# GNN layer on one core: the second lane's sort placed behind the first lane's matmuls, sums stored by SyncE, the quad loop written out

## The chip, the core and the metric

The kernel runs on one core of a Trainium2 chip. The metric is the device time of one execution in microseconds (us). The kernel before took 24514.12 us (median of ten runs, 24499.75 to 24533.43). A difference of 0.2% is about what these runs can tell from no change.

## The reference

A graph layer over V = 100,000 nodes with 64 features and 3,300,000 edges (`src`, `dst`, sorted by `dst`, self loops included):

```python
h = jnp.maximum(_layernorm(x, axis=-1), 0.0)
local = features[tgt]; nbr = features[src]          # features = h
y = concat([local, nbr - local], -1) @ W.T + b
s = segment_sum(y, tgt);  cnt = segment_sum(1, tgt)
x = x + where(cnt > 0, s / maximum(cnt, 1), 0)
```

Since the map is linear, what has to be made per node is the sum of `h[src]` over its edges and the number of edges; the matrix is applied afterwards, once per node.

## The kernel before

**Stages.** (1) Preparation: layer norm of all nodes; each row of h is stored in DRAM as three bf16 parts and two ones (`h3`, 194 columns, 388 bytes), and a sum table `acc` is zeroed. (2) Edge sums, two ways at once, added into `acc`. (3) Per node: mean, matrix, output (lines 976 to 1019).

**Way one, chunks** (`chunks`, L343 to 412): 352 chunks of 128 x 28 edges. For each of the 28 columns one indirect DMA on GpSimd (POOL), a "gather", brings 128 rows of `h3` into a tile `nb` (L391): 9856 gathers in all. VectorE (DVE) makes one-hots `hot` of the edges' targets, 14 columns at a time and 128 targets wide (L340 through `one_hot`), and TensorE (PE) multiplies them with the rows, one matmul for each gather (L396), into 128 node sums. DVE takes the sums out (L407, L409), and POOL adds them to `acc` in DRAM: with an indirect DMA (L366) before the loop and with a direct accumulating DMA (L371) inside it.

**Way two, windows and quads.** The other 2,039,808 edges lie in 256 windows of 7968 edges, each over at most 256 neighbouring targets. Four windows make a quad; 32 quads (128 windows, one per partition) make a lane; there are two lanes, so 64 quads. For a lane, `sort_lane` (L413 to 617) sorts the keys of each partition by source block: pieces of up to 1536 key pairs, each a copy on ScalarE (ACT) into a PSUM tile `tmp` (L455), then a minimum and a maximum on DVE (L456, L457). `fill_lane` (L620 to 738) then fetches the sorted keys in small pieces with 225 POOL gathers (L636, L721), and DVE and ACT turn them into index tables in DRAM. `quads` (L740 to 881) works through 157 source blocks of 640 rows for each quad, two blocks at a step, 79 steps a quad: SyncE (SP) loads the block table `tab` (L761, 727.5 KB for three blocks) and the indices `srs`, `dt`; DVE makes the one-hots `gh` (L789) and `dh` (L340); PE picks rows out of the block (`pick`, 12 matmuls a step, L811); ACT moves them to SBUF (`gs`, L813); PE adds them up by target (`put`, 32 small matmuls a step, L819). At a quad's end ACT and DVE make four tiles `wsums` (L835 to 845), and POOL adds them to `acc` with accumulating DMAs (L849).

**What sets the order.** Instructions are ordered on each engine by a scheduler that takes the earliest written instruction that is ready; `issue_after` holds one behind another. Work is interleaved by Python generators: `gathers(ns)` emits one gather for each `GATHER` = 1250 ns of credit (`took()` takes credit off for a gather of `fill_lane`). Lane 0 is sorted with gathers beside it; lane 1 is sorted with gathers and lane 0's fill beside it; quads 0 to 3 run with lane 1's fill and gathers; `drain(ev)` finishes the first 58 chunks (L909); then a hardware loop (`For_i`, L911) runs three times over 20 quads and 98 chunks. An addition to `acc` isn't issued at once: `add_later` files it, and `add_now` issues it some gathers later (56 gathers, then at least `GAP` = 8 apart). A register for its address is first loaded on the issuing engine (`number`, L318).

Of the kernel before, what the change touches and what calls it, by code (L numbers as in the profile page):

```python
# [32 lines left out]
LANES = 2  # L33
SB = 20
KB = 98
U0 = 4
KG = 16
# [3 lines left out]
STEP = 1050  # L41
GAP = 8
# [19 lines left out]
PIECE = 1536  # L62
COUNTS = 1
GAIN = 2.0 ** 40
PART = 1024
# [19 lines left out]
def plan(v, e):  # L85

    wl = 1 << int(np.log2(33 * CH * 1.05))
    ew = wl - PAD
    nw = LANES * P
    chunks = -(-(e - nw * ew) // CHUNK)  # L90
    return wl, nw, max(chunks, (nw // W - U0) // SB * KB)


@with_exitstack
def gnn_preln(ctx: ExitStack, tc, x, src_w, dst_w, src_p, dst_p, src_a, dst_a, wT, b, out, V, E):
# [27 lines left out]
    SETS = NL * G  # L123
# [7 lines left out]
    PA = NCH - (SETS - U0) // SB * KB  # L131
# [4 lines left out]
    assert 2 * C == P and NCB % 2 == 1 and PA >= 0 and SL % 2 == 0  # L136
# [9 lines left out]
    wb_d = dram.tile([SETS * W, 1], I32, name="wb_d")  # L146
# [28 lines left out]
    wb_r = consts.tile([1, SETS * W], I32, name="wb_r")  # L175
    turns = consts.tile([1, 2], I32, name="turns")
    ones = consts.tile([P, 1], F32, name="ones")
# [4 lines left out]
    odd = consts.tile([P, 1 + 5 * LANES], F32, name="odd")  # L182
# [22 lines left out]
    with tc.tile_pool(name="pre", bufs=2) as pre, tc.tile_pool(name="small", bufs=4) as small, \  # L205
# [32 lines left out]
        most = small.tile([P, NMT], F32, name="most", bufs=1)  # L238
        nc.vector.memset(least, 0.0)
        nc.vector.memset(most, 0.0)  # L240

        def bounds(m):
# [3 lines left out]
            nc.vector.tensor_reduce(least[:n, m:m + 1], d[:n], axis=AX.X, op=ALU.min)  # L246
            if m == NMT - 1:

                nc.vector.scalar_tensor_tensor(d[:n], d[:n], float(V), d[:n], op0=ALU.is_lt, op1=ALU.mult)
            nc.vector.tensor_reduce(most[:n, m:m + 1], d[:n], axis=AX.X, op=ALU.max)  # L250
            if m < NMT - 1:
                return
            span = small.tile([P, NMT], F32, name="span", bufs=1)
            nc.vector.tensor_sub(span, most, least)
            nc.vector.tensor_reduce(odd[:, 0:1], span, axis=AX.X, op=ALU.max)
            nc.vector.tensor_scalar(odd[:, 0:1], odd[:, 0:1], float(P), None, op0=ALU.is_ge)
# [55 lines left out]
    with tc.tile_pool(name="rows", bufs=6) as rows, \  # L312
# [5 lines left out]
        def number(at, engine, most):  # L318
            with tc.issue_after(last[engine].ins):
                return nc.values_load(at, engines=[engine], min_val=0, max_val=most)  # L320
# [5 lines left out]
        later = []  # L326
        count = [0, 0]
# [4 lines left out]
        def add_now(all_of_them=False):  # L332
            while later and (all_of_them or (later[0][0] <= count[0] and count[0] - count[1] >= GAP)):
                later.pop(0)[1]()
                count[1] = count[0]

# [8 lines left out]
        def chunks(first, n, dynamic=None):  # L345


            def load(q):
# [7 lines left out]
                nc.vector.tensor_sub(rel[:, :k], di[:, :k], base_b[:, at][:, :, None].to_broadcast([P, k, J]))  # L356
                near = index.tile([P, KG, J, D], I16, name="near")
                nc.vector.tensor_scalar(near[:, :k], rel[:, :k, :, None].to_broadcast([P, k, J, D]), float(2 * CH), None,
                                        op0=ALU.min)
                to = index.tile([P, KG], I32, name="to", bufs=3)  # L360
                nc.vector.tensor_scalar(to[:, :k], base_b[:, at], pcol, None, op0=ALU.add)
                return si, near, to

            def addition(q, rows_to, sums):
                if dynamic is None:
                    nc.gpsimd.indirect_dma_start(  # L366
                        out=acc, out_offset=bass.IndirectOffsetOnAxis(ap=rows_to, axis=0),
                        in_=sums, in_offset=None, compute_op=ALU.add)
                else:
                    at = number(base_r[0:1, ds(dynamic + q, 1)], POOL, V)  # L370
                    nc.gpsimd.dma_start(acc[ds(at, P)], sums, accum_op=ALU.add)  # L371

            ahead = load(0)
            before = None
            parts = J // JH
            for k in range(n * parts + 1):
                q, part = divmod(k, parts)
                u = q % KG
                if q < n:
                    if u == 0 and part == 0:  # L380
                        si, near, to = ahead
                    hot = rows.tile([P, JH, P], BF16, name="hot", bufs=4)
                    nb = rows.tile([P, JH, CT], BF16, name="nb")
                    with behind():
                        one_hot(hot, near[:, u, part * JH:part * JH + JH], P)
                if before is not None and before[2] == 0:
                    ps = rows_ps.tile([P, CE], F32, name="ps")
                for j in range(JH):
# [6 lines left out]
                    if before is not None:  # L395
                        nc.tensor.matmul(ps, lhsT=before[0][:, j], rhs=before[1][:, j, :CE],  # L396
# [7 lines left out]
                if before is not None and before[2] == parts - 1:  # L404
                    sums = rows.tile([P, C1], F32, name="sums", bufs=LAG + 2)
# [4 lines left out]
                    add_later((LAG - 1) * J, lambda b=before[3], s=sums: addition(*b, s))  # L410
                if q < n:
                    before = (hot, nb, part, (q, to[:, u:u + 1]))
# [5 lines left out]
        def sort_lane(l, keys, piece, few, ps):  # L418

            whole = keys.bitcast(I32)  # L420
# [3 lines left out]
            nc.vector.tensor_scalar_min(wb[:, 0:1], wb[:, 0:1], float(V - CH))  # L424
            last[DVE] = nc.vector.tensor_reduce(wb[:, 1:2], whole[:, :EW], axis=AX.X, op=ALU.max)
# [6 lines left out]
            mine = slice(l * P, l * P + P)  # L432
            for i in range(W):
                nc.sync.dma_start(wb_d[mine].rearrange("(g i) o -> i g o", i=W)[i], wb_i[i * G:i * G + G])
            nc.sync.dma_start(wb_r[:, mine], wb_d[mine].rearrange("w o -> o w"))
            for a in range(0, EW, PART):
# [12 lines left out]
                last[DVE] = nc.vector.scalar_tensor_tensor(d, d, 1, s[:, :n],  # L449
                                               op0=ALU.logical_shift_left, op1=ALU.bitwise_or)  # L450
# [3 lines left out]
            def exchange(lo, hi, tmp):  # L454
                last[ACT] = nc.scalar.copy(tmp, lo)  # L455
                nc.vector.tensor_tensor(lo, tmp, hi, ALU.min)  # L456
                last[DVE] = nc.vector.tensor_tensor(hi, tmp, hi, ALU.max)  # L457
# [601 lines left out]
```

## Time and profile before

| What | us |
|---|---|
| Median of ten runs | 24514.12 |
| The profiled execution: its time | 24535.56 |
| Its span in the trace | 24533.9 |
| Lane 0's sort: first key fetch of its fill | 1649 |
| First `gh` one-hot of quad 0 | 2726 |
| First and last quad sums before the loop | 3290, 4080 |
| First gather sums added inside the loop | 4379 |
| Last quad's sums taken out of PSUM | 24196 |
| End of the span | 24534 |

The trace is read in windows of time. In each, a row gives the busy time of each engine with the number of its instructions in brackets, then the TensorE clock that was granted (1 is full), the busy share of the DMA engines and GB/s. PE is matmuls, PEld weight loads. A group row gives the line, the engine, the operation, the number of instructions, busy time and mean ns of one, and, after the bar, the idle time of the engine just before them with what ended it. "issue" means that nothing that the profile shows was being waited for.

### The profile page before, as it was taken

What the parts mean: (1) busy time and instruction counts of PE and PEld (TensorE: products, weight loads), DVE (VectorE), ACT (ScalarE), POOL (GpSimd) and SP (SyncE); (2) the same over time, 40 slices, a digit from 0 to 9 for tenths busy, and PEclk for the clock granted to TensorE, in tenths of its full rate; (3) what the DMA queues carried; (4) which work ended last, traced back from release to release, by engine and by line L of the source; (5) the groups of instructions that cost most, each with busy time, mean ns of one, the idle gap of its engine ahead of it and who ended that gap; (6) DMA issues with size and microseconds to landing.
All of it is one profiled execution on the core that took longest, in us unless ns stands there. A gap on an engine that the chain in (4) does not pass through costs nothing. (4 is left out here: it accounts for less than half of the span.)

```text
span 24533.9 us, 559362 instructions
## 1 busy us (share of the span) xinstructions
PE 15201.9 (62%) x238778; PEld 10912.5 (44%) x238778; DVE 11304.8 (46%) x15452; ACT 6034.7 (25%) x11710; POOL 11122.7 (45%) x11210
## 2 busy tenths in 40 slices
PE   4100365666666666657666666666576666766666
PEld 3000244444444444445444444444454444444445
DVE  6879543444444444434444444444344444444444
ACT  4333321222222222222222222222222222222222
POOL 5666534444444444434444444444344444444444
PEclk6555577777777777777777777777777777777777
DMA  6612364555555555555555555555555555555557
GB/s 234 102 43 48 102 176 149 174 176 175 175 172 175 175 178 174 175 158 180 175 175 176 176 171 175 175 175 176 159 180 174 175 176 175 175 177 176 173 174 252
DMA packets 1746424, 4097.89 MB, mean 167 GB/s; under 512 B 943899, under 2 KB 952230, under 8 KB 1738950
## 3 DMA queue, kind: packets, MB, share of 16 engines
q1 hardware_dynamic: 1182534, 3461.26, 41.7%
q0 software_dynamic: 454208, 535.92, 11.1%
q10 hardware_dynamic: 107168, 64.74, 1.2%
q8 instruction: 1877, 30.75, 0.5%
q14 instruction: 637, 5.22, 0.1%
HBM read 3880.72 MB, written 219.04 MB: 167 GB/s over the span
## 5 line engine op out<-in xcount | busy, mean ns | idle before, releaser
L391 POOL DMA_INDIRECT nb<-h,si x9856 | 9421.0, 956 | 11738.0 <-PE ps L396 8031.2
L819 PE MATMUL total<-gs,dh 32*128 32x193 bf16 x160768 | 6608.8, 266 | 4278.0 <-issue 4254.3
L340 DVE TENSOR_TENSOR dh<-dt,c 128x1024 bf16<-128x1024 int16 x5056 | 3451.5, 683 | 11992.5 <-remote 7483.2
L813 ACT CAST gs<-gp 128x386 bf16<-128x386 f32 x10048 | 4761.2, 482 | 16234.3 <-remote 9614.5
L811 PE MATMUL gp<-tab,gh 128*128 128x193 bf16 x60288 | 7498.7, 274 | 1976.7 <-issue 1751.6
L811 PEld LDWEIGHTS <-gh 128*128 128x128 bf16 x60288 | 5490.3, 106 | 3666.4 <-issue 3242.8
L819 PEld LDWEIGHTS <-dh 32*128 32x128 bf16 x160768 | 3943.3, 99 | 6624.1 <-issue 6562.4
L789 DVE TENSOR_TENSOR gh<-srs,c 128x1536 bf16<-128x1536 int16 x5056 | 4764.2, 942 | 23.9 <-issue 18.3
L396 PE MATMUL ps<-nb,hot 128*128 128x193 bf16 x9856 | 1940.6, 280 | 2633.4 <-DVE sums L409 1220.7
L396 PEld LDWEIGHTS <-hot 128*128 128x128 bf16 x9856 | 1045.9, 111 | 2808.2 <-DVE sums L409 1252.9
L455 ACT COPY tmp<-keys 128x1536 f32<-128x1536 f32 (+14 forms) x540 | 649.9, 1213 | 1281.2 <-issue 568.5
L456 DVE TENSOR_TENSOR keys<-tmp,keys 128x1536 f32<-128x1536 f32 (+14 forms) x540 | 757.0, 1423 | 88.0 <-ACT junk L533 35.9
L457 DVE TENSOR_TENSOR keys<-tmp,keys 128x1536 f32<-128x1536 f32 (+14 forms) x540 | 757.1, 1422 | 14.0 <-remote 7.1
L340 DVE TENSOR_TENSOR hot<-near,c 128x1792 bf16<-128x1792 int16 x704 | 760.2, 1080 | 2.8 <-PE ps L396 2.7
L849 POOL DMA_DIRECT2D acc<-wsums x256 | 347.4, 1357 | 326.9 <-DVE wsums L845 219.0
L636 POOL DMA_INDIRECT kf<-ksort,at_i x322 | 309.1, 960 | 200.1 <-ACT k L677 105.4
L371 POOL DMA_DIRECT2D acc<-sums x294 | 300.9, 1023 | 209.9 <-DVE sums L409 200.6
L839 DVE SCALAR_TENSOR_TENSOR whole<-own,whole 128x193 f32<-128x193 bf16 x512 | 191.2, 416 | 178.5 <-ACT whole L835 178.0
L778 POOL DMA_INDIRECT rows_x<-h,xs x128 | 123.3, 963 | 324.7 <-DMA xs<-xs_d 262.0
L407 DVE TENSOR_REDUCE sums<-ps 128x64 f32<-128x192 f32 x352 | 123.8, 352 | 226.9 <-remote 168.5
L303 PE MATMUL o_ps<-w_own,hT 128*128 128x128 f32 x784 | 186.3, 376 | 15.1 <-ACT hT L298 14.6
L303 PEld LDWEIGHTS o_ps<-w_own,hT 128*128 128x128 f32 x784 | 154.9, 252 | 80.9 <-ACT hT L298 71.1
(174 smaller groups left out, 3522.4 us busy)
## 6 DMA issues: line engine op xcount, KB each, us to landing
tab<-tables SPq DMA_DIRECT2D x3328, 727.5 KB
srs<-sr_d SPq DMA_DIRECT2D x1216, 512.0 KB
nb<-h,si POOLq DMA_INDIRECT x9856
tables<-h ACTq DMA_DIRECT2D x157, 242.5 KB
h<-parts SPq DMA_DIRECT2D x28, 1358.0 KB
acc<-zeros SPq DMA_DIRECT2D x28, 910.0 KB
at<-acc SPq DMA_DIRECT2D x28, 910.0 KB
xt<-in_x SPq DMA_DIRECT2D x28, 896.0 KB
```

What stands on the lines that cost most here:

```text
L303: nc.tensor.matmul(o2[:, i], lhsT=hT[:, i], rhs=w_own.rearrange("p a c -> p (a c)"), start=False, stop=True)
L340: nc.vector.tensor_tensor(out.rearrange("p k (a d) -> p k a d", d=D), numbers[:, :, None].to_broadcast(shape), upto[:shape[0], :n].rearran ...
L391: last[POOL] = nc.gpsimd.indirect_dma_start(out=nb[:, j], out_offset=None, in_=h3, in_offset=bass.IndirectOffsetOnAxis(ap=si[:, u, at:at + ...
L396: nc.tensor.matmul(ps, lhsT=before[0][:, j], rhs=before[1][:, j, :CE], start=before[2] == 0 and j == 0, stop=before[2] == parts - 1 and j ...
L455: last[ACT] = nc.scalar.copy(tmp, lo)
L456: nc.vector.tensor_tensor(lo, tmp, hi, ALU.min)
L457: last[DVE] = nc.vector.tensor_tensor(hi, tmp, hi, ALU.max)
L789: nc.vector.tensor_tensor(gh[:, :m].rearrange("p c i b s -> p (c i) b s"), srs[u, s // SL][:, c:c + m].rearrange("p c i s -> p (c i) s")[: ...
L811: nc.tensor.matmul(gp[:, i], lhsT=ghots[t][:, i, b], rhs=row[:, b + i * (NB - NR), :CE], start=b == 0, stop=b == NR - 1)
L813: nc.scalar.copy(gs[t], gp)
L819: nc.tensor.matmul(total[:, i, to(b)], lhsT=hot[at, b * P:b * P + P], rhs=of[at], start=flags.get("start", False) and b == 0, stop=flags.g ...
L849: nc.gpsimd.dma_start(acc[ds(at, CH)].rearrange("(b p) c -> p b c", p=P), sums, accum_op=ALU.add)
```

## The change

- **Sums are stored, not accumulated.** `keep` replaces `addition`: SP stores the sums of a chunk or window to `acc` with a plain DMA (`put`), and at least four gathers later copies the one row that the next chunk or window will overwrite to a side table (`shared`, DRAM to DRAM). At the end five indirect accumulating DMAs add the side rows back (`add_side`); the first three chunks' sums are kept in SBUF and added by POOL at the end.
- **Lane 1 is sorted and filled behind lane 0's 32 quads** (`behind_quads`): each step takes a unit of it. Pieces are up to 1024 keys, `tmp` is one tile in SBUF, and the copy is written two steps ahead of its minimum and maximum. Lane 0's fill starts just ahead of quad 0 and goes on beside it.
- **All 64 quads are written out**: 32, then 32. No `For_i`.
- **A fifth of the block tables** (11 of 53) is loaded once into SBUF for the second 32 quads.
- **Chunk one-hots are 32 columns wide** instead of 128, written on a diagonal into four tiles zeroed once; each gather's 128 edges are now neighbours in the sorted list (the host transposes the chunks).
- Sizes: `nb` buffers 6 to 5, `wsums` 8 to 5, index loads of 8 chunks instead of 16, `dh` 3 to 5 buffers with the end one-hots cut into pieces of its size; a few more DVE operations in `bounds` and at the end.

```diff
+PARTS = (32, 32)
+U1 = 32
-KG = 16
+KG = 8
-STEP = 1050
-GAP = 8
+STEP = 2200
+BEHIND = 1.0
+BAND = 32
+GAP = 4
+EARLY = 3
+KEEP = 5
-PIECE = 1536
+PIECE = (1536, 1024)
-PART = 1024
+PART = 512
...
-    with tc.tile_pool(name="rows", bufs=6) as rows, \
+    with tc.tile_pool(name="rows", bufs=5) as rows, \
...
-            def addition(q, rows_to, sums):
-                if dynamic is None:
-                    nc.gpsimd.indirect_dma_start(
-                        out=acc, out_offset=bass.IndirectOffsetOnAxis(ap=rows_to, axis=0),
-                        in_=sums, in_offset=None, compute_op=ALU.add)
-                else:
-                    at = number(base_r[0:1, ds(dynamic + q, 1)], POOL, V)
-                    nc.gpsimd.dma_start(acc[ds(at, P)], sums, accum_op=ALU.add)
-
+            def keep(q, sums):
+                c = ds(first + q if dynamic is None else dynamic + q, 1)
+                after = ds(first + q + 1 if dynamic is None else dynamic + q + 1, 1)
+
+                def put():
+                    at = number(base_r[0:1, c], SP, V)
+                    last[SP] = nc.sync.dma_start(acc[ds(at, P)], sums)
+
+                def shared():
+                    at = number(base_r[0:1, after], SP, V)
+                    last[SP] = nc.sync.dma_start(side_c[c], acc[ds(at, 1)])
+
+                add_later((LAG - 1) * J, put)
+                add_later((LAG - 1) * J + GAP, shared)
...
-                    hot = rows.tile([P, JH, P], BF16, name="hot", bufs=4)
+                    hot = narrow[part][q % 2]
...
-                        one_hot(hot, near[:, u, part * JH:part * JH + JH], P)
+                        one_hot(hot[:, part * JH * D:][:, :JH * (P + D)].rearrange("p (k x) -> p k x", x=P + D)[:, :, :BAND],
+                                near[:, u, part * JH:part * JH + JH], BAND)
...
             def exchange(lo, hi, tmp):
-                last[ACT] = nc.scalar.copy(tmp, lo)
-                nc.vector.tensor_tensor(lo, tmp, hi, ALU.min)
-                last[DVE] = nc.vector.tensor_tensor(hi, tmp, hi, ALU.max)
+                ins = nc.scalar.copy(tmp, lo)
+                if not soft:
+                    last[ACT] = ins
+
+                def finish():
+                    nc.vector.tensor_tensor(lo, tmp, hi, ALU.min)
+                    ends_at(nc.vector.tensor_tensor(hi, tmp, hi, ALU.max))
+
+                return finish
+
+            def both(part, n):
+                finish = part()
+                if soft:
+                    yield 0
+                    yield 0
+                finish()
+                yield 2.083 * n + 290
...
-                if s < NCB and s % TG == 0:
+                if s < NCB and s % TG == 0 and kept is not None and s // TG % KEEP == 0:
+                    tabs[u, s // TG] = kept[:, s // TG // KEEP]
+                elif s < NCB and s % TG == 0:
...
-                    sums = load.tile([P, NT, C1], F32, name="wsums", bufs=8)
+                    sums = load.tile([P, NT, C1], F32, name="wsums", bufs=5)
...
-                    def addition(w=(base + u) * W + i, sums=sums):
-                        at = number(wb_r[0:1, ds(w, 1)], POOL, V - CH)
-                        nc.gpsimd.dma_start(acc[ds(at, CH)].rearrange("(b p) c -> p b c", p=P), sums, accum_op=ALU.add)
-
-                    add_later((LAG - 1) * J, addition)
+                    keep(u, i, sums)
...
-            ev = chunks(0, PA)
+            ev = chunks(0, NCH)
...
+                with tc.tile_pool(name="load", bufs=3) as load, tc.tile_pool(name="hots", bufs=3) as hots, \
+                        tc.tile_pool(name="tmp", bufs=1) as tmp, tc.tile_pool(name="g_ps", bufs=2, space=PSUM) as g_ps, \
+                        tc.tile_pool(name="a_ps", bufs=1, space=PSUM) as a_ps:
+
+                    def behind_quads():
+                        for l in range(1, NL):
+                            yield from sort_lane(l, keys(), piece, few, tmp)
+                            yield from fill_lane(l, fill, took)
+
+                    begin = fill_lane(0, fill, took)
+                    for _ in range(4 * SL):
+                        next(begin)
+                    rest = behind_quads()
+                    left = 0.0
+                    for i, _ in enumerate(quads(0, U1, late=True)):
+                        if i < NE // 2 - 10:
+                            for _ in range(4):
+                                next(begin, None)
+                            gathers(STEP / 2)
+                        else:
+                            drain(begin)
+                            left += BEHIND
+                            while left > 0:
+                                left -= 1 + next(rest, 0) / 1500
+                            gathers(STEP)
                     drain(rest)
+                    add_now(True)
...
+                kept = stay.tile([P, -(-NTB // KEEP), TG, NB, CT], BF16, name="kept")
...
+                pace = (NCH * J - count[0]) / ((SETS - U1) * NE // 2 - 4)
+                owed = 0.0
+                for _ in quads(U1, SETS - U1, kept):
+                    gathers(pace * GATHER)
                 drain(ev)
                 add_now(True)
-                with tc.For_i(0, (SETS - U0) // SB, 1) as g:
-                    ev = chunks(None, KB, PA + g * KB)
-                    next(ev)
-                    owed = 0.0
-                    for _ in quads(U0 + g * SB, SB):
-                        owed += 2 * (KB * J - 1) / (SB * NE)
-                        while owed > 0:
-                            next(ev, None)
-                            owed -= 1
-                    drain(ev)
-                    add_now(True)
+                last.clear()
+                for q, sums in enumerate(early):
+                    at = number(base_r[0:1, q:q + 1], POOL, V)
+                    nc.gpsimd.dma_start(acc[ds(at, P)], sums, accum_op=ALU.add)
...
+        def add_side(k, rows_of, to, a, z):
+            of = few.tile([P, C1], F32, name="side", bufs=NMT + SETS * W // P)
+            at = few.tile([P, 1], I32, name="side_at", bufs=NMT + SETS * W // P)
...
+            nc.gpsimd.indirect_dma_start(out=acc, out_offset=bass.IndirectOffsetOnAxis(ap=at, axis=0),
+                                         in_=of, in_offset=None, compute_op=ALU.add)
```

## The prediction

> **What bounds the kernel now.** I read the page's slices first. They say that no engine is full for most of the run:
>
> ```profile
> PE   4100365666666666657666666666576666766666
> DVE  6879543444444444434444444444344444444444
> POOL 5666534444444444434444444444344444444444
> ```
>
> PE works six to seven tenths of the quads' time, DVE and POOL four. DVE is full only in slices 1 to 4: that is the two sorts, with PE nearly idle. So I asked the view of waits what PE waits for:
>
> ```profile
> PE total L819 <- issue: 4397.0, 6332, 3.2
> PE gp L811 <- issue: 1751.6, 2400, 33.3
> PE gp L811 <- DMA tab<-tables: 69.9, 64, 13.4
> ```
>
> It waits for nothing that the profile shows: 6149 us of "issue", 70 us for block tables. To see when, I cut a piece of the loop into two windows (columns: stretch, length, PE, PEld, DVE, ACT, POOL busy with counts, clock, DMA share, GB/s):
>
> ```profile
> 8010.00:8016.00 6.00, 6.00 (x138) 5.05 (x136) 4.33 (x7) 2.75 (x7) 0.00 (x0) 1.00 0.78 254
> 8020.00:8032.00 12.00, 6.54 (x76) 3.34 (x71) 2.55 (x4) 1.49 (x4) 9.03 (x10) 0.76 0.64 172
> ```
>
> With POOL silent, PE makes 138 matmuls in 6 us; a step is 46 (32 put, 12 pick, 2 chunk), so a step takes about 2.0 us. With POOL issuing DMAs back to back it makes 76 in 12 us, and nobody is waited for. PE's instructions come slowly while POOL writes DMAs. The price follows from two stretches of 750 us, where the groups by line count 228 steps (`gh`, L789) in 3250 to 4000 and 177 in 6000 to 6750:
>
> ```profile
> 3250.00:4000.00 750.00, 572.35 (x10392) 426.91 (x10387) 385.31 (x537) 219.52 (x463) 245.72 (x247) 0.81 0.67 213
> 6000.00:6750.00 750.00, 510.60 (x8226) 362.40 (x8217) 310.01 (x434) 169.39 (x360) 325.72 (x338) 0.75 0.56 175
> ```
>
> POOL's column counts its DMAs: 247/228 = 1.083 a step at 3.289 us a step, and 338/177 = 1.910 at 4.237 us. The slope is 0.948/0.827 = **1.147 us for each POOL DMA**, the rest **2.05 us a step**, which is the rate read above with POOL silent. Test on the whole loop: 60 quads x 79 steps x 2.05 + 1.147 x (8232 gathers + 120 `rows_x` + 294 + 240 additions) = 9717 + 10192 = 19909; the loop ran from 4380 to 24196, 19816. So the quads are bound by the sum of PE's work and POOL's DMAs, and those DMAs are free only where PE has nothing to do: in the sorts.
>
> At one place a page of the Trainium skill differs. "Runtime: NRT & Kernel Launch", section "Instruction fetch mechanics", says that the sequencer streams its instructions by its own DMA queue in 16 KiB blocks and that this is mostly hidden. The page's instruction queue here moved 30.75 MB in 1877 packets, which is 16 KB each, but the 6149 us of "issue" aren't hidden. By that rule POOL's DMAs would cost PE nothing and the quads would stay at 4.18 us a step (21130 us); I go by the slope.
>
> **The change, part by part.**
>
> *Lane 1's sort goes behind the quads.* Now lane 0's first key fetch is at 1649 and quad 0's first one-hot at 2726: 1077 us for lane 1, with PE idle. Afterwards quad 0 follows lane 0. Lane 0's sort itself shrinks: lane 1's first reading no longer lies in it (8 blocks x 5.9 us of L443 to L449 and 17 us of reductions, some 64 us of DVE, which is 85% busy there), some 50 chunk one-hots get shorter by 0.69 us (35 us; slope of the one-hot rows: 1024 elements 686 ns, 512 elements 421, so 448 elements 0.39 us against 1.08), while `bounds` (about ten DVE passes at 3.7 us, estimated from 1792 elements in 2.0 us) and blocks of 512 add as much. With 30 us for the first fetches, quads start at 1649 - 64 + 30 = **1615**.
>
> *POOL DMAs beside the quads.* Removed: 256 window and 352 chunk additions. But gathers move in. Before, 45 + 743 + 487 = 1275 ran ahead of 2726 (group L391 by windows); now only lane 0's sort is ahead. Its credit, in the code's own terms, is 8 x 7968 + 2.083 x 327679 + 270 x 290 + 74 x 700 ns = 876 us, over 1250 ns: 701 gathers. Beside the quads: 9856 - 701 = 9155, fills 450 less 24, 128 `rows_x`: 9709. Before, from 2726 on: 8581 + 225 + 128 + 256 + 294 + 28 = 9512. So storing by SP roughly pays for the gathers that lost the second sort's cover; it is no gain by itself. Quads: 64 x 79 x 2.05 + 1.147 x 9709 = 10365 + 11136 = 21501; scaled by the loop's test (19816/19909) 21400, and I take **21450**. That compares with 21470 from 2726 to 24196 before, in which 300 us (4080 to 4380) went to draining gathers with no quads beside them.
>
> *Lane 1's sort on DVE and ACT.* 339 pieces; L456 and L457 take 1.22 us at 1024 elements and 0.72 at 512, so 797 us; with reading and fill some 1060 us of DVE. By the units that the code counts (1667 for the sort, 360 for the fill) this ends at step 2030 of 2459, so nothing is left over after quad 31. DVE's own work is 1.8 us a step; with the sort 2.3, against a mean step of 4.2. In PE's fast stretches (2.05 a step) that is too much, but DVE is two to three steps ahead after each of POOL's bursts. Bounds: below, -100 us (shorter `hot`, 0.09 us a step, should a fast stretch now wait for DVE); above, half of the 1060 us falls into fast stretches, +530. I take +60 with ACT's copies, near the lower end, because quad 0 ran with a whole lane's fill beside it in 564 us, and the formula (79 x 2.05 + 1.147 x 275 POOL DMAs = 477, plus the start) nearly explains that alone.
>
> *`tmp` in SBUF.* Now the minimum reads one PSUM operand. Gathers beside such pieces keep their 0.94 us; beside an operation with two SBUF inputs they don't:
>
> ```profile
> 832.08 0.94 POOL L391 DMA_INDIRECT nb<-h,si  x1 [0.30 <-issue]
> ...
> 834.17 1.22 DVE L443 TENSOR_TENSOR own<-s,keys 128x1024 int32<-128x1024 int32 x1
> 834.57 1.63 POOL L391 DMA_INDIRECT nb<-h,si  x1 [0.30 <-issue]
> ```
>
> Over the 28 gathers that overlap L443 the mean is 1.37 us instead of 0.95. POOL gathers for 0.43 of the time, so of 678 operations 290 meet one: 290 x 0.41 = 120 us of POOL, **+110 to +135**; ends 0 and 678 x 1.2 = 810.
>
> The page "SBUF — State Buffer", section "SBUF: two separate sides", speaks against the change in the same way: DVE with two SBUF inputs and GpSimd exclude each other for a whole instruction. By it each meeting could cost the whole operation: 290 x 1.2 = 350 us.
>
> *SP's stores.* 605 pairs. Each operation costs SP a register load (0.27 us), register arithmetic and the issue (0.3 to 0.4), some 1.2 us as in the loads of `own` (L767). `shared` waits for `put` to land; the accumulating stores landed in 3.4 us (L849, median of issue to landing). Behind it on SP are the next block tables, and PE waits for those. Four gathers lie between, about 2.2 steps or 4.6 us, so mostly nothing is waited for: I take +40. Below: 0; above: in the rival.
>
> *The rest.* Quad 0 needs lane 0's whole fill before its end (64 small gathers after 36 us of DVE): +60. Between quads 31 and 32 the pipeline empties and 8 MB of resident tables are loaded first, 11 x 727.5 KB at some 200 GB/s = 40 us: +60. Resident tables save a fifth of the table traffic in the second half, where PE waits 70 us for tables in all: 0 (it could give 50). End: 24196 to 24534 is 338, and the last stores, three early sums and five side additions run one after another. The last additions before came every 3.6 us, so about 14 more of these: +50. One-hots on the diagonal leave PE's matmuls as they are: 0; the cover is PE's order, and its price if gone is in the DVE bounds.
>
> Sum: 1615 + 21450 + 130 + 60 + 40 + 60 + 60 + 338 + 50 = 23803 for the span. The profiled execution is 20 us above the median; I also take 40 off for the tables and shorter one-hots: **23740**, 3.2% less.
>
> **Rivals.**
> 1. *DVE sets the pace in the first half.* The scheduler takes any ready instruction, so the sort may be packed into few quads. For: `tmp` has one buffer and nothing holds the sort back. Against: quad 0 before. Price: up to 530: 24270.
> 2. *SP holds up the tables: slower.* Place: `shared` waits on SP in front of L761. A pair that waits for both landings blocks SP for about 8 us, a step's cover is 4.6. Decides from (24514 - 23740)/605 = 1.3 us of PE stall a pair. At 2.5: 25250. For: SP already waits 6793 us for table buffers, so a table is asked for late. Against: only 70 us of PE's waits are tables.
> 3. *Better than that.* The two-input collisions are rare and fast stretches gain from the lighter DMA load: 23400.
> 4. *It doesn't do what it says.* The sort isn't done by quad 31 and drains alone: the 1077 us come back: 24800.
>
> **How the numbers follow.** Forecast (23500 to 24000) 0.60; rival 3 0.10; rival 1 0.15; rival 2 0.10; rival 4 0.05. The range 23300 to 24450 takes in the forecast, rival 3 and most of rival 1, with the bounds of DVE and of the collisions but not of SP. 0.2% (49 us) is what a measurement can tell. Faster: 0.60 + 0.10 + 0.14 = 0.84; same 0.03, out of rivals 1 and 4; slower 0.13.
>
> **What would show it.** Right: first `gh` near 1615; 5056 steps in about 21600 us; about 9709 POOL DMAs beside them; PE's wait still "issue"; L371, L366 and L849 gone from POOL. Lane 1's minima spread over most of quads 1 to 25. Wrong: `gp <- tab` in the hundreds of us (rival 2), PE waiting for `gh` or `dh` (rival 1), gathers beside L456 far above 1 us, or a slope other than 1.147 once additions are gone, for then POOL's DMAs aren't what slows PE.

## The result and the profile after

The changed kernel takes 25585.26 us (median of 8 runs, 25563.05 to 25601.85) against 24521.82 us before (28 runs). The ratio is 1.0434, 95% interval 1.0424 to 1.0443: 4.3% slower, where 3.2% faster was forecast. The profiled execution has a span of 25585.1 us.

The page's slices (40 equal parts of the span, busy tenths):

```profile
PE   4135664666666666666666666666666666666666
...
DVE  6868763333333334443333333333333333333333
...
POOL 5651335333333333333334444444444444444444
```

Each slice is 640 us. DVE's slices 4 to 6 (8, 7 and 6 tenths, with PE at 5 and 6) are lane 1's sort, which before lay in front of PE's work. So the change did what it says. In slice 7, where POOL is at 5 with lane 1's fill, PE falls to 4; from slice 8 on it stays at six tenths, and that part is now longer.

The view of waits (us in total, times, longest):

```profile
PE total L880 <- issue: 4326.5, 5760, 3.2
...
PE gp L872 <- issue: 3118.7, 4056, 5.0
...
PE gp L872 <- DMA tab<-tables: 184.8, 131, 6.2
```

PE's "issue" waits rose from 6149 us to 4326.5 + 3118.7 = 7445 us. Block tables cost 185 us instead of 70. The new SP traffic isn't what holds PE up.

Two neighbouring windows of the changed kernel (columns as before: PE, PEld, DVE, ACT, POOL with counts, clock, DMA share, GB/s), one with a run of 14 gathers and one without:

```profile
8051.90:8069.10 17.20, 7.49 (x79) 3.33 (x67) 2.67 (x4) 1.07 (x3) 13.09 (x14) 0.70 0.48 159
8069.10:8086.20 17.10, 15.10 (x296) 12.44 (x299) 9.97 (x14) 6.46 (x14) 0.04 (x1) 0.80 0.55 186
```

The picture is the one that the prediction started from: 79 matmuls in 17.2 us beside gathers, 296 in the next 17.1 us without them. What has changed is how often PE gets through a run with so little, and that comes out of the experiments.

### The profile page after: what moved, and what is told of

Read it like the earlier page. It is cut to its first block, busy times and chain, and to the rows that moved or that the text cites. A ratio compares the mean times of both kernels' runs of the same rounds, so it can differ in the third digit from the quotient of the medians.

```text
span 25585.1 us, 554527 instructions
## 1 busy us (share of the span) xinstructions
PE 15445.7 (60%) x238778; PEld 10951.6 (43%) x238778; DVE 10945.6 (43%) x15750; ACT 6072.6 (24%) x11927; POOL 10319.9 (40%) x10611
## 5 line engine op out<-in xcount | busy, mean ns | idle before, releaser
L872 PE MATMUL gp<-tab,gh 128*128 128x193 bf16 x53952 | 7073.5, 276 | 3566.1 <-issue 2759.7
L880 PE MATMUL total<-gs,dh 32*128 32x193 bf16 x160768 | 6444.1, 269 | 4109.8 <-issue 4092.6
L880 PEld LDWEIGHTS <-dh 32*128 32x128 bf16 x165888 | 4048.3, 101 | 6427.8 <-issue 6363.8
L872 PE MATMUL gp<-kept,gh 128*128 128x193 bf16 x6336 | 870.1, 278 | 408.5 <-issue 358.9
L495 ACT COPY tmp<-keys 128x1024 f32<-128x1024 f32 (+15 forms) x609 | 671.9, 1111 | 1254.5 <-DVE keys L501 682.1
L500 DVE TENSOR_TENSOR keys<-tmp,keys 128x1024 f32<-128x1024 f32 (+15 forms) x609 | 773.4, 1280 | 89.8 <-ACT tmp L495 49.4
L501 DVE TENSOR_TENSOR keys<-tmp,keys 128x1024 f32<-128x1024 f32 (+15 forms) x609 | 775.7, 1283 | 14.8 <-DVE keys L500 0.5
L360 DVE TENSOR_TENSOR dh<-et,c 128x1024 bf16<-128x1024 int16 (+1 forms) x192 | 114.8, 598 | 579.4 <-remote 388.9
L360 DVE TENSOR_TENSOR hot<-near,c 128x448 bf16<-128x448 int16 x704 | 268.6, 381 | 0.0
L896 ACT COPY whole<-total 128x388 f32<-128x388 f32 x256 | 105.0, 497 | 340.4 <-PE total L880 280.8
```

Of the source, the lines that this page charges most:

```text
L360: nc.vector.tensor_tensor(out.rearrange("p k (a d) -> p k a d", d=D), numbers[:, :, None].to_broadcast(shape), upto[:shape[0], :n].rearran ...
L495: ins = nc.scalar.copy(tmp, lo)
L501: ends_at(nc.vector.tensor_tensor(hi, tmp, hi, ALU.max))
L872: nc.tensor.matmul(gp[:, i], lhsT=ghots[t][:, i, b], rhs=row[:, b + i * (NB - NR), :CE], start=b == 0, stop=b == NR - 1)
L880: nc.tensor.matmul(total[:, i, to(b)], lhsT=hot[at, b * P:b * P + P], rhs=of[at], start=flags.get("start", False) and b == 0, stop=flags.g ...
```

## Reading the price of a gather and of an addition again

The changed kernel makes no additions beside its quads. So its trace gives the price of a gather and of a step without them, from two stretches of 4000 us. First POOL's groups in 6000 to 10000, then DVE's `gh`, of which there is one a step:

```profile
L421 POOL DMA_INDIRECT nb<-h,si x1579 | 1489.8, 943 | 2352.6 <-PE ps L426 1902.8 <-issue 440.0 <-DMA nb<-h,si 9.7
L835 POOL DMA_INDIRECT rows_x<-h,xs x24 | 22.6, 942 | 135.6 <-PE total L880 132.0 <-issue 3.7
```

```profile
L846 DVE TENSOR_TENSOR gh<-srs,c 128x1536 bf16<-128x1536 int16 (+1 forms) x912 | 864.6, 948 | 2281.6 <-remote 1207.8 <-PE gp L872 1056.6 <-issue 14.0
```

The same groups in 14000 to 18000:

```profile
L421 POOL DMA_INDIRECT nb<-h,si x1720 | 1622.6, 943 | 2279.9 <-PE ps L426 1792.3 <-issue 476.7 <-DMA nb<-h,si 11.0
L835 POOL DMA_INDIRECT rows_x<-h,xs x20 | 18.9, 944 | 79.7 <-PE total L880 70.4 <-remote 6.3 <-issue 3.0
```

```profile
L846 DVE TENSOR_TENSOR gh<-srs,c 128x1536 bf16<-128x1536 int16 x833 | 790.3, 949 | 2391.1 <-remote 1340.5 <-PE gp L872 1022.6 <-issue 27.9
```

With I for a step and g for a gather, 4000 = 912 I + 1603 g and 4000 = 833 I + 1740 g. This gives g = **1.256 us** and I = **2.18 us**. A third stretch, 10000 to 12000, has 508 steps and 702 gathers: 508 x 2.18 + 702 x 1.256 = 1988 of 2000 us. SP's stores go along with steps and gathers in these stretches, so whatever they cost is inside the two prices.

Now the kernel before in 6000 to 10000:

```profile
L391 POOL DMA_INDIRECT nb<-h,si x1658 | 1582.0, 954 | 2182.3 <-PE ps L396 1559.6 <-issue 461.5 <-DMA si<-in_src_p 107.4
L849 POOL DMA_DIRECT2D acc<-wsums x48 | 65.5, 1365 | 43.7 <-DVE wsums L845 27.7 <-DVE dh L340 12.8 <-DVE gh L789 2.3
L371 POOL DMA_DIRECT2D acc<-sums x60 | 61.5, 1026 | 0.3
L778 POOL DMA_INDIRECT rows_x<-h,xs x24 | 23.3, 970 | 39.8 <-DMA xs<-xs_d 33.5 <-issue 5.7 <-DMA nb<-h,si 0.6
```

```profile
L789 DVE TENSOR_TENSOR gh<-srs,c x951: 547/947/957, 6002.7 to 9996.1; 128x1536 bf16<-128x1536 int16 x189, 128x768 bf16<-128x768 int16 x2
```

Steps and gathers alone, at those prices, would take 951 x 2.18 + 1682 x 1.256 = 4184 us. The stretch is 4000 us long, and it also holds 108 additions. So an addition didn't cost 1.147 us. It was worth about -1.7 us. That is arithmetic across two programs, not a proof; the runs below test it. One of them, the kernel before without additions (e3), has 921 steps and 1628 gathers in the same stretch, 4051 us at these prices. So about 0.5 of the 1.7 us may be a difference between the two programs.

## The experiments

Each run is compared with the kernel before on the same chip. This matters here more than usual: on three chips the kernel before takes 24512 to 24844 us, as in the result, and on two others 15384 to 15396 us. I call them chips of the first and the second kind; more on them at the end. The cause of the result can only be read on the first kind.

| Label | What it is | Median us | Before, same chip | Ratio (95%) |
|---|---|---|---|---|
| first kind | | | | |
| e1_put_pool | POOL issues the stores | 25382.31 | 24511.66 | 1.0358 (1.0341 to 1.0376) |
| e2_half_runs | runs of 7 gathers | 25181.38 | 24511.66 | 1.0269 (1.0252 to 1.0286) |
| e3_before_no_add | before without additions | 25050.18 (one run) | 24511.66 | 1.022, no interval |
| c_after | the change again | 25930.82 | 24843.70 | 1.0443 (1.0425 to 1.0460) |
| e5c_sorts_first | sort not hidden | 25568.31 | 24843.70 | 1.0295 (1.0278 to 1.0312) |
| e10b_both | sort not hidden, additions back | 24739.97 | 24843.70 | 0.9959 (0.9945 to 0.9973) |
| e11b_early | e10, additions early in a run | 24251.01 | 24843.84 | 0.9765 (0.9748 to 0.9781) |
| e12b_late | e10, additions last in a run | 25145.45 | 24843.84 | 1.0124 (1.0107 to 1.0141) |
| second kind | | | | |
| e5, e5b | sort not hidden | 16155.17, 16136.00 | 15383.99, 15396.13 | 1.0501, 1.0480 |
| e6, e6b | before written out | 15737.06, 15753.54 | 15383.99, 15396.13 | 1.0232, 1.0230 |
| e9_add_on_pool | additions back, sort hidden | 16706.78 | 15396.13 | 1.0853 (1.0835 to 1.0871) |
| e10_both | sort not hidden, additions back | 16034.21 | 15396.13 | 1.0416 (1.0398 to 1.0433) |
| e11_early, e12_late | place of the additions | 15910.49, 15855.85 | 15389.32 | 1.0345, 1.0304 |

The theory at the outset (A) was that PE gets its instructions only while no gather is on its way, so that the number and shape of the runs of gathers decides. Rival B was SP: its stores and copies hold up the tables.

**e1: the stores go to POOL.** `put` is issued by POOL as a plain DMA, `shared` stays on SP.

```diff
-                    at = number(base_r[0:1, c], SP, V)
-                    last[SP] = nc.sync.dma_start(acc[ds(at, P)], sums)
+                    at = number(base_r[0:1, c], POOL, V)
+                    nc.gpsimd.dma_start(acc[ds(at, P)], sums)
```

> The kernel after, with the 605 stores of sums (put) issued by POOL again, as plain DMAs, each with its register load on POOL; the copies to the side table (shared) stay on SP. Theory A (an unbroken run of 14 gathers on POOL cuts PE off from its 16 KB instruction blocks; anything else on POOL between gathers breaks the run and lets a block through): faster than the kernel after by 500 to 1000 us, 24600 to 25100. Theory B (SP's stores hold up the block tables): 100 to 300 us faster, since half of SP's operations are gone. The prediction's price (1.147 us for each POOL DMA, whatever it is): 605 x 1.147 = 690 us slower, 26280.

Measured: 25382 us, 200 us faster than the change. 605 more POOL DMAs made the kernel faster; the prediction's price, 1.147 us for each, would have made it 700 us slower. Theory A had expected more; rival B's 100 to 300 us fits as a number, but PE's waits for block tables are 175 us here and 185 in the change, so the tables aren't where the 200 us come from.

**e2: runs of 7 gathers.** `JH` = 7 instead of 14, twice as many `nb` buffers.

> The kernel after with tiles of 7 gathers instead of 14 (JH = 7) and 10 of them instead of 5: the same gathers and matmuls, but POOL's runs end after 7 gathers (8.7 us). Theory A: in the trace PE makes about 62 matmuls in the first 8.7 us of a run and only 12 in the second half, so two short runs carry some 50 matmuls more than a long one; 650 runs x 50 / 17 a us = 1900 us less at best, 23700 to 24600. Theory B and the prediction's price: nothing changes, 25500 within 100.

Measured: 25181 us, 400 us faster. Theory A's 23700 to 24600 is missed by far. Between 6000 and 24000 a run of 7 carries 64 matmuls in 8.6 us, as A said, but between the runs PE makes 13.2 matmuls a us instead of the change's 16.4.

**e3: the kernel before without its additions.** Both `addition` functions return at once, so the edge sums are missing from its output.

> The kernel before without its additions to the sum table (the 608 POOL DMAs of L366, L371 and L849 and their register loads are left out, so the output lacks the edge sums). Theory A: the additions had broken POOL's runs; without them all runs are of 14 gathers with 74 matmuls instead of 111 on average, 575 runs x 37 / 17 a us = 1250 us lost, less the 400 to 860 us of POOL time that goes: 24900 to 25400, slower although work is gone. The prediction's price: 578 x 1.147 = 660 us faster, 23860. Theory B says nothing about it: between.

Measured: 25050 us, 540 us slower than before, with 608 POOL DMAs fewer and no stores on SP in their place. It is a single run, but its trace bears it out: its 466 runs of 14 gathers carry 78 matmuls on average. This refutes the price on which the prediction's sum was built: work taken away cost time.

**e5 and e6: undo the sort alone; write out the kernel before.** e5 sorts both lanes ahead of the quads as before (gathers beside both sorts, fill of lane 0 beside lane 1's sort) and keeps the rest of the change. e6 is the kernel before without `For_i` and without the lone `drain(ev)`.

```diff
-            soft = l > 0
+            soft = False
...
-                    begin = fill_lane(0, fill, took)
...
+                rest = fill_lane(NL - 1, fill, took)
+                for _ in quads(0, U1):
+                    gathers(STEP)
+                    next(rest, None)
```

```diff
-            ev = chunks(0, PA)
+            ev = chunks(0, NCH)
...
-                drain(ev)
-                add_now(True)
-                with tc.For_i(0, (SETS - U0) // SB, 1) as g:
+                pace = (NCH * J - count[0]) / ((SETS - U0) * NE // 2 - 4)
+                owed = 0.0
+                for _ in quads(U0, SETS - U0):
+                    gathers(pace * GATHER)
```

> The changed kernel, except that both lanes are sorted before the quads, with chunk gathers beside both sorts and lane 0's fill beside the second, as in the kernel before. Theory A (a gather costs PE 1.0 to 1.3 us wherever PE has work, so what the second sort covered was worth nearly what it cost): quads start 1093 us later, but 491 chunk gathers and 225 fill gathers less lie beside the quads (716 x 1.2 = 860 us) and the sort's own 410 us beside the first quads are gone: 25400 (25250 to 25550). The prediction's prices (1.147 a gather, sort 60 + 130): 1093 - 821 - 190 = 80 us slower than the changed kernel, 25670. Rival B (the loss lies in the written out program, not in the sort): within 50 us of the changed kernel.

> The kernel before with all its 64 quads and 352 chunks written out: no hardware loop, no gathers finished alone ahead of it; additions stay on POOL. Theory A: the gathers that were finished alone in 300 us now lie beside quads at about the same price, so little is won: 24300 to 24550. Rival B (a written out program is fetched more slowly than a loop): 25000 or more. The prediction's prices: those gathers at 1.147 us beside quads, 24450.

> The kernel of e5 again, for a chip where the kernel before takes 24500 us; expected there as before: Theory A 25400 (25250 to 25550), the prediction's prices 25670, rival B 25535 to 25635. Where it takes 15400 us: 16155 again.

> The kernel of e6 again, for a chip where the kernel before takes 24500 us; expected there as before: Theory A 24300 to 24550, rival B 25000 or more, the prediction's prices 24450. Where it takes 15400 us: 15737 again.

> The changed kernel with both lanes sorted before the quads, again, for a chip where the kernel before takes 24500 us. Theory A 25400 (25250 to 25550), the prediction's prices 25670, rival B (the loss is in the written out program) 25535 to 25635. Where it takes 15400 us: 16140 again.

e5 and e6 ran on chips of the second kind, twice, and e5 a third time (e5c) on one of the first. There it took 25568 us beside the change's 25931: undoing the sort gives 363 us back. Theory A had expected 185, the prediction's prices a loss of 85. The line of `gh` (one for each step, first and last start) shows where it comes from. The change on that chip (c_after):

```profile
L846 DVE TENSOR_TENSOR gh<-srs,c x5056: 547/955/964, 1622.2 to 25506.4; 128x1536 bf16<-128x1536 int16 x192, 128x768 bf16<-128x768 int16 x3
```

e5c:

```profile
L846 DVE TENSOR_TENSOR gh<-srs,c x5056: 546/955/967, 2711.1 to 25156.6; 128x1536 bf16<-128x1536 int16 x192, 128x768 bf16<-128x768 int16 x3
```

Quads start 1089 us later, and end sooner all the same. The quads take 1440 us less than in the change (from first `gh` to last sums 23902 and 22462 us). 669 gathers that no longer lie beside quads account for 669 x 1.256 x 1.0135 = 852 us of this (1.0135 is the chip's own slowness, from c_after's stretch), and some 590 us are left for the sort and for whatever else the prices miss.

e6 never ran on a chip of the first kind, so what writing out the loop does there stays open. On the second kind it costs 2.3%.

**e7, e8, e9, e10: additions back on POOL.** e9 is the change with accumulating additions in place of stores, copies and the five side additions. e10 is e5 with the same edit.

```diff
-                    at = number(base_r[0:1, c], SP, V)
-                    last[SP] = nc.sync.dma_start(acc[ds(at, P)], sums)
+                    at = number(base_r[0:1, c], POOL, V)
+                    nc.gpsimd.dma_start(acc[ds(at, P)], sums, accum_op=ALU.add)
...
-                add_later((LAG - 1) * J + GAP, shared)
```

> The changed kernel with POOL's direct accumulating additions back in place of SP's stores, copies of shared rows and the side additions at the end. Theory A (an accumulating DMA among the gathers costs PE nothing, and lets it catch up: the kernel before lost 540 us when it lost 608 of them): 605 additions, 400 to 700 us faster than the changed kernel, 24900 to 25200. Rival C (only the break in the run of gathers counts, whatever breaks it: plain stores on POOL gave 200): 25350 to 25450. The prediction's price, 605 x 1.147 = 690 us less 40 for SP's stores and 50 for the tail: 26180.

> The changed kernel with both sorts first and POOL's accumulating additions back: what stays of the change is the written out loop, the 32 column one-hots, the resident tables. Theory A: the two gains add up, 25585 - 180 - 600 = 24800 (24600 to 24950). Rival C: 25200. Rival B: 25400 or more. The prediction's prices: 26250.

In e7 and e8 the kernel's own test for overlapping sums took the first chunk into account and sent both through the fallback over all edges: 164041 and 163419 us, which say nothing on the question. e9 and e10 leave that test out.

> The changed kernel with POOL's direct accumulating additions back in place of SP's stores, copies of shared rows and the side additions at the end (its check for overlapping ranges of sums is taken out too). On a chip where the kernel before takes 24500 us. Theory A (an accumulating DMA among the gathers costs PE nothing, and lets it catch up: the kernel before lost 540 us when it lost 608 of them): 605 additions, 400 to 700 us faster than the changed kernel, 24900 to 25200. Rival C (only the break in the run of gathers counts, whatever breaks it: plain stores on POOL gave 200): 25350 to 25450. The prediction's price, 605 x 1.147 = 690 us less 40 for SP's stores and 50 for the tail: 26180. On a chip where the kernel before takes 15400 us, gathers do not slow PE, and hiding the sort should lose: 16650.

> The changed kernel with both sorts first and POOL's accumulating additions back (without its check for overlapping ranges of sums): what stays of the change is the written out loop, the 32 column one-hots, the resident tables. Where the kernel before takes 24500 us: Theory A, the two gains add up, 25585 - 180 - 600 = 24800 (24600 to 24950); Rival C 25200; Rival B (the loss lies in the written out program) 25400 or more; the prediction's prices 26250. Where it takes 15400 us: 16000, from the time of its last quad in the run that went on into the fallback.

> The changed kernel itself once more, beside the two below. Where the kernel before takes 24500 us: 25585 as measured. On a chip where it takes 15400 us, gathers do not slow PE; the kernel with the sort hidden and POOL's additions took 16707 there, and taking those additions off POOL should matter little: 16800 (16600 to 16950), so that the change loses there too.

> Both sorts first and POOL's accumulating additions back, again, for a chip where the kernel before takes 24500 us. Theory A 24800 (24600 to 24950), rival C 25200, rival B 25400 or more, the prediction's prices 26250. Where it takes 15400 us: 16034 again.

On one chip of the first kind: the change 25931, sort undone 25568, additions back as well 24740. So the additions that SP took over are worth **828 us**, 1.37 us each; rival C's number (200 us) and the prediction's sign are both out. So is rival B: PE's waits for block tables are 215 us in e5c and 160 in e10b, 55 us of the 828. Another 37 us lie behind the last sums (369 us to the end in e5c, 332 in e10b), where the side additions are gone. The rest of the change (loop written out, narrow one-hots, resident tables) is a gain: 0.4% faster than before. On the second kind, e9 against e10 says that hiding the sort costs 670 us there too; the additions matter little (16034 against 16136).

**e11 and e12: where in a run the addition stands.** In the kernel before, the trace's runs of 14 gathers (between 6000 and 24000) with one addition as the third or fourth DMA carry 139 matmuls on average (180 runs), those with it in place 8 or 9 carry 103 (17 runs), runs without one 76 (186). In e10b, whose additions often come last, the runs with one at the end carry 70 (206 runs), those without one 80 (211) and those with two or more 200, in 21.5 us (76). So e11 issues additions only behind the third gather of a run, and e12 only behind the last.

```diff
-                        add_now()
+                        if j == 2:
+                            add_now()
```

(e12: `if j == JH - 1:`.)

> The kernel of e10 (both sorts first, accumulating additions on POOL), with additions issued only behind the third gather of a run of 14, so one a run at most. Theory A2 (where the kernel before takes 24500 to 24850 us an accumulating DMA early in a run lets PE's instructions come in the middle of it: in the kernel before, runs with one behind gathers 1 to 6 carry 135 to 139 matmuls, pure runs 76; in e10, where 42% of the runs have theirs at the end, those carry 70): 23600 to 24300. Rival C2 (an addition helps wherever it stands, by some time that POOL waits): 24650 to 24850, as e10. Where the kernel before takes 15400 us: 16000 to 16100, no effect.

> The kernel of e10 with additions issued only behind the last gather of a run. Theory A2: they give nothing there, so it is as without additions in the runs, the time of e5 on such a chip less the tail: 25300 to 25600. Rival C2: 24650 to 24850. Where the kernel before takes 15400 us: 16000 to 16100.

> The kernel of e11 again, for a chip where the kernel before takes 24500 to 24850 us: Theory A2 23600 to 24300, rival C2 24650 to 24850 (as e10). Where it takes 15400 us: 15910 again.

> The kernel of e12 again, for a chip where the kernel before takes 24500 to 24850 us: Theory A2 25300 to 25600, rival C2 24650 to 24850. Where it takes 15400 us: 15856 again.

On the first kind: 24251 us early, 25145 us late, 24740 anywhere (e10b). The same DMAs, the same number, and 894 us between two places. Rival C2 falls. A2's number for early holds; for late it was 25300 to 25600, so that against e5c late additions are still worth some 400 us, in which SP's stores and the side additions have gone too. On the second kind the place hardly matters (15910 and 15856). One run of e11b and the window behind it:

```profile
8102.20:8120.90 18.70, 11.15 (x162) 7.07 (x150) 4.69 (x8) 2.55 (x6) 14.63 (x15) 0.81 0.59 149
8120.90:8135.10 14.20, 12.64 (x220) 10.07 (x224) 8.40 (x12) 5.10 (x11) 0.11 (x1) 0.76 0.65 217
```

POOL in that run, from its third gather (start, length, line; the addition stands fourth):

```profile
8104.81 0.94 POOL L420 DMA_INDIRECT nb<-h,si  x1 [0.31 <-issue]
8105.75 1.38 POOL L916 DMA_DIRECT2D acc<-wsums  x1
8107.44 1.06 POOL L420 DMA_INDIRECT nb<-h,si  x1 [0.30 <-issue]
```

One run of e12b and the window behind it:

```profile
8057.30:8075.70 18.40, 7.49 (x79) 3.70 (x79) 2.88 (x6) 0.96 (x2) 14.19 (x15) 0.66 0.46 129
8075.70:8093.10 17.40, 15.15 (x302) 12.15 (x306) 10.21 (x14) 6.64 (x14) 0.27 (x1) 0.86 0.74 224
```

162 matmuls in 18.7 us with the addition early, 79 in 18.4 us with it last, which is what the change's run without one had (79). Over all runs between 6000 and 24000: some 470 early ones carry 139 on average, some 430 late ones 76. With the prices above (times 1.0135 for these chips), 4000 us of e11b hold 953 steps, 1698 gathers and 107 additions at -2.5 us; of e10b 925, 1650 and 107 at -1.3; of e12b 907, 1629 and 103 at -0.7.

## Why the prediction was wrong

**The bound: right in kind.** PE waits for its instructions while gathers are written; SP didn't become the bound (rival 2: 185 us of table waits), and DVE at most in the five quads that hold the sort (rival 1, below); rival 4 is out, since the sort ended long before quad 31.

**The step that failed: "The slope is 0.948/0.827 = 1.147 us for each POOL DMA".** It gave one price to gathers and additions alike. POOL's groups in its two windows, 3250 to 4000 first:

```profile
L391 POOL DMA_INDIRECT nb<-h,si x223 | 212.8, 954 | 500.5 <-PE ps L396 437.1 <-issue 61.2 <-DMA nb<-h,si 1.8
L849 POOL DMA_DIRECT2D acc<-wsums x12 | 16.4, 1370 | 4.4 <-DMA acc<-wsums 2.5 <-DVE dh L340 1.6 <-DVE whole L839 0.3
L366 POOL DMA_INDIRECT acc<-sums,to x8 | 13.0, 1629 | 2.4 <-issue 2.1 <-DVE dh L340 0.3
L778 POOL DMA_INDIRECT rows_x<-h,xs x4 | 3.8, 960 | 31.5 <-PE total L819 30.9 <-issue 0.6
```

and 6000 to 6750:

```profile
L391 POOL DMA_INDIRECT nb<-h,si x314 | 299.5, 954 | 415.3 <-PE ps L396 295.2 <-issue 87.4 <-DMA si<-in_src_p 30.5
L371 POOL DMA_DIRECT2D acc<-sums x12 | 12.3, 1023 | 0.0
L849 POOL DMA_DIRECT2D acc<-wsums x8 | 10.9, 1364 | 4.1 <-DVE dh L340 4.1
L778 POOL DMA_INDIRECT rows_x<-h,xs x4 | 4.0, 988 | 5.0 <-DMA xs<-xs_d 4.1 <-issue 0.9
```

These are 227 gathers (`rows_x` among them) and 20 additions, and 318 gathers and again 20 additions. With equal numbers of additions, the difference of the windows says nothing on them; the price of an addition was assumed, and it fixed the scale of the other two. Leave it open, as a: the windows then give 2.11 - 0.056 a for a step and 1.18 - 0.032 a for a gather, and the prediction's test on the whole loop gives 19890 + 4 a. So that test comes out for nearly any a and couldn't find the mistake. With a = -1.7 the windows give 2.21 and 1.24, close to what the changed kernel gave. The runs showed 1.256 us for a gather, 2.18 us for a step instead of 2.05, and -0.9 to -1.7 us for an addition (taking them away costs 540 us for 608 in e3 and 828 for 605 in e5c against e10b; -1.7 is the arithmetic above). With the corrected prices the quads' term is 5056 x 2.18 + 9622 x 1.256 = 23107 us instead of 21450. That is some 1660 of the 1780 us by which the span was missed, and it turns "storing by SP roughly pays for the gathers that lost the second sort's cover" around: both parts cost. The prediction had named a slope other than 1.147 as a sign that POOL's DMAs aren't what slows PE. The slope came out as 1.256, and gathers do slow PE; it is the additions that don't.

**Start of the quads, counts: right.** First `gh` 1622.5 (1615 predicted); 9072 chunk gathers and 9622 POOL DMAs beside the quads (9155 and 9709).

```profile
L846 DVE TENSOR_TENSOR gh<-srs,c x5056: 546/954/965, 1622.5 to 25199.6; 128x1536 bf16<-128x1536 int16 x192, 128x768 bf16<-128x768 int16 x3
```

**Lane 1's sort: mis-sized.** Its terms were 60 us on DVE and 130 for `tmp`, with 160 more for SP's stores, quad 0's fill and the gap between the halves. All five come to 350; measured 23595 (first `gh` to last sums) - 23107 = 488 us here, and some 590 by e5c. "Spread over most of quads 1 to 25" was wrong. The minima of lane 1 in the changed kernel (339, first and last start):

```profile
L500 DVE TENSOR_TENSOR keys<-tmp,keys x339: 152/1216/2046, 1962.6 to 3725.3; 128x1024 f32<-128x1024 f32 x72, 128x1008 f32<-128x1008 f32 x21, 128x1020 f32<-128x1020 f32 x17, 128x960 f32<-128x960 f32 x13
```

They run from 1963 to 3725, which is five quads; the scheduler took them early. That stretch has 363 steps and 496 gathers, 1414 us at the prices above, so 349 us are left for the sort against 190 predicted. Rival 1 had named this, at up to 530 us.

**Two SBUF operands: smaller than feared.** Gathers beside the sort (1640 to 3300):

```profile
L421 POOL DMA_INDIRECT nb<-h,si x266 | 269.9, 1015 | 556.2 <-PE ps L426 456.3 <-issue 98.7 <-DMA nb<-h,si 1.2
```

1015 ns against 943 in 6000 to 10000: 0.07 us on 266 gathers, about 20 us there, not 110 to 135. Over the whole sort 263 of POOL's DMAs overlap one of its 678 operations (290 predicted) and take 1.08 us on average, the others 0.95: some 35 us. The page "SBUF — State Buffer" of the Trainium skill, section "SBUF: two separate sides", as the prediction used it, would have given 350; these rows show neither.

**Small terms.** The end took 368 us after the last sums (388 predicted). One-hots of 448 elements take 381 ns (0.39 predicted) and gained nothing that shows.

## What to carry to other kernels

A slope from two windows prices only what differs between them: if a third kind of work is equally frequent in both, its price is assumed, not read, and a test on the whole that has the same mix can't find out. Before hiding idle work behind a busy stage, ask what that idle time already covers: lane 1's sort had some 670 of POOL's DMAs for company, and hiding it made each of them cost 1.26 us. The place of an instruction in a queue can be worth more than its removal (894 us between two places, 540 and 828 for removal).

## What the runs showed of the hardware

**An accumulating DMA early in a run of gathers speeds PE up.** It costs POOL 1.03 or 1.37 us and a gap of 0.30, and yet gives PE some 65 matmuls more in that run. By the trace, 16 KB packets of PE's instruction queue start 0.9 times in a run of 17 us without one (kernel before, 186 runs), 0.73 of them in its first 5 us, and 1.45 times in e11b's runs, 0.72 in the first 5 us. A plain store does nearly the same in the same place: the 17 of e1's runs that have theirs fourth carry 127 matmuls, against 139 with an accumulating one. But most single stores of e1 stand elsewhere: ahead of the first gather (86 runs, 103 matmuls), in place 6 or 7 (31 runs, 85) or in the last five (85 runs, 73). So e1's 200 us against e10b's 828 are at least in part a matter of place; how much the accumulating adds by itself stays open.

**Chips differ.** On the second kind of chip a run of gathers doesn't slow PE. e5b, a run of 14 gathers and the window behind it:

```profile
8117.30:8134.40 17.10, 14.95 (x337) 12.52 (x326) 11.71 (x17) 6.74 (x14) 12.93 (x14) 1.00 0.82 248
8134.40:8141.40 7.00, 2.29 (x28) 1.66 (x29) 1.12 (x2) 0.96 (x2) 0.26 (x1) 0.74 0.91 294
```

337 matmuls in 17.1 us, at a clock of 1.00; the changed kernel's run on the first kind had 79 at 0.70. Over e5b's 125 runs between 6000 and 24000 it is 302 in 17.4 us, with 2.4 packets of PE's instruction queue in each. In e5b PE waits for block tables instead:

```profile
PE gp L872 <- DMA tab<-tables: 1628.2, 702, 18.0
...
PE total L880 <- issue: 40.3, 58, 2.0
```

The "issue" ahead of the put matmuls is 40 us there, against 4326 in the changed kernel on the first kind. So the Trainium skill's "mostly hidden", said of the crossing from one block of instructions to the next ("Runtime: NRT & Kernel Launch", section "Instruction fetch mechanics"), agrees with the second kind and not with the first. The changed kernel itself didn't run on the second; by e9 and e10 its main step, the hidden sort, loses there as well. What makes two chips differ so much in the same program no run here can say. The version with early additions beats both kernels on the first kind (0.9765, 0.9748 to 0.9781), and loses to the kernel before on the second (1.0345).
